# Lines layer of a four-layer scan stack: one padded copy by rows and one by columns, in place of one by rows for each of two images

## The chip, the cores and the metric

The kernel runs on one core of a Trainium2 chip. The metric is the device time of one launch, in microseconds. The kernel before takes 17721.58 us, the median of three runs that lie between 17714.92 and 17727.33 us.

## What is computed

The input is eight images of 48 x 48 pixels and 96 channels, float32. Four layers follow each other; each adds a function of the group-normed input to its input. Layers 0 and 3 are selective-scan blocks with a 3 x 3 convolution, layer 1 is a pointwise network between an up- and a downsampling, and layer 2, called the lines layer here, is the one that the change touches. It runs four independent scan blocks over the lines of the image: its rows forward, its rows backward, its columns forward and its columns backward.

```python
def _scan_block(x, in_w, conv_w, conv_b, xproj_w, dt_w, dt_b, A_log, D, outp_w):
    xz = x @ in_w
    xi, z = jnp.split(xz, 2, axis=-1)
    xc = jnp.pad(xi, ((0, 0), (K - 1, 0), (0, 0))).transpose(0, 2, 1)
    xconv = conv_general_dilated(xc, conv_w[:, None, :], ...)   # 4 taps along the line, per channel
    xi = jax.nn.silu((xconv + conv_b[None, :, None]).transpose(0, 2, 1))
    x_dbl = xi @ xproj_w
    dt_low, Bm, Cm = jnp.split(x_dbl, [DT_RANK, DT_RANK + D_STATE], axis=-1)
    dt = jax.nn.softplus(dt_low @ dt_w + dt_b)
    A = -jnp.exp(A_log)
    y = _selective_scan(xi, dt, A, Bm, Cm, D)    # h = exp(dt A) h + dt B u;  y = C h + D u
    y = y * jax.nn.silu(z)
    return y @ outp_w

b, h, w, c = x.shape
x_hf = x.reshape(b * h, w, c)
x_hb = x_hf[:, ::-1]
x_v = x.transpose(0, 2, 1, 3).reshape(b * w, h, c)
x_vb = x_v[:, ::-1]
ys = jax.vmap(_scan_block)(jnp.stack([x_hf, x_hb, x_v, x_vb]), in_w, conv_w, ...)
# the four results are turned back, concatenated and multiplied by out_w; out_b is added
```

Here x has been group-normed (32 groups of three channels), there are 192 inner channels and 16 states, and the result is added to the layer's input.

## The kernel before, in words

The program works through layer 0, then layer 2, then layer 3, each image by image. Layer 1 has no stretch of its own: as a "guest" it is strewn in small pieces into the slots of layers 0 and 2.

In the lines layer (`lines`, from line 772) channels lie on the partitions. An image is taken in four directions, k = 0 and 1 along rows, k = 2 and 3 along columns, and each direction in five blocks of ten lines (the last of eight), 480 or 384 positions. So an image is 20 blocks. A block is eight slots, or four turns of two slots. In a turn VectorE (DVE) runs three scans (L331) over 128 partitions x 2 x 480 positions. ScalarE (ACT) makes their decays with an exp (`make_da`, L323), and copies of B into PSUM (L280). VectorE and GpSimd (POOL) multiply `dt u` by B (L299), GpSimd multiplies the scanned states by C (L337), and TensorE (PE) sums them over states into `ps_y` (`reduce`, L357 and L359). When a half's `ps_y` is complete, VectorE multiplies it by the gate (`done`, L919), TensorE projects it (L928) and VectorE adds it to the image in SBUF (L934, L936).

What a block needs before its scans is made ahead, by `stage1`, three blocks early. The dictionary at its end says in which slot each step is issued; counted from the start of the block two before it, the convolution of the first half is in slot 3, of the second half in slot 4, and the gate's matmuls (`s7`, L897) in slot 1 of the next block. ACT has silus in slots 6 and 2 and a softplus in slot 0, each with a table load, and one more to return to exp.

The convolution and the input projection are one: four matmuls, one for each tap, read the normed image at four offsets (L854), and the gate reads it at offset zero (L897). A float32 matmul is two instructions in the profile. For that the normed image lies in `xpad`, with three zeros between lines of 48 (`step` is 51) and three lines of zeros above and below. There are two such tiles, for even and odd images, both laid out by rows. Where the direction is along columns, `shifted` turns the view around:

```python
def shifted(off):
    v = shift(xp, off, 0).rearrange("p h w -> p w h") if col else shift(xp, 0, off)
    return v[:, b.r0:b.r0 + b.nr, :]
```

so that neighbouring positions lie 51 elements apart.

The order of every engine's work is written out by hand; no scheduler moves it. In each slot `aside` issues, in this order: loads of B, C and dt, one step of `side`, the steps of `stage1`, postponed steps, and a piece of the guest. `side(job)` prepares the next image: in slot 8 of an image (or later, if layer 1 has not finished the next one) it issues the load of the next image on SyncE's queue, 28 slots later it starts `front`, whose statistics (`norm_scale`, L191 to L214) take 15 slots, and then writes the padded copy with five ACT instructions (L177), one per slot: slots 51 to 55 of 160. `load_x` uses two tiles in turn, so an image is loaded over the one before the present one. An image's result is stored by L938 after its last block.

Of the kernel before, what the change touches and what calls it, by code (L numbers as in the profile page):

```python
# [10 lines left out]
AF = mybir.ActivationFunctionType  # L11
# [4 lines left out]
H, W, C = 48, 48, 96  # L16
# [3 lines left out]
NK = 4  # L20
# [4 lines left out]
BLKS = [(0, 10), (10, 10), (20, 10), (30, 10), (40, 8)]  # L25
# [4 lines left out]
NG = 8  # L30
# [24 lines left out]
def seq(t, col):  # L55

    if len(t.shape) == 2:
        return t.rearrange("p (h w) -> p w h" if col else "p (h w) -> p h w", w=W)
    return t.rearrange("p a (h w) -> p a w h" if col else "p a (h w) -> p a h w", w=W)
# [42 lines left out]
def vss_stack_kernel(ctx: ExitStack, tc: tile.TileContext, i: dict, out: bass.AP):  # L102
    nc = tc.nc
# [11 lines left out]
    def weights(pool, names):  # L115
        w = {}
        for name in names:
            shape = list(i[name].shape)
            w[name] = pool.tile(shape, F32, tag=f"w_{name}", name=f"w_{name}")
            nc.sync.dma_start(w[name], i[name])  # L120
        return w
# [49 lines left out]
    def group_norm(x, into, psum, behind=lambda step: step()):  # L171


        got = {}
        yield from norm_scale(x, got, psum, behind)
        for r0, nr in BLKS:
            nc.scalar.activation(into(r0, nr), x[:, r0:r0 + nr, :], AF.Identity, bias=got["shift"], scale=got["rs"])  # L177
            yield True

    def norm_scale(x, got, psum, behind=lambda step: step()):  # L180


        def mean_of(v):
            def run():
                got["p"] = psum()
                nc.tensor.matmul(got["p"][:C, :1], lhsT=wc["gmat"], rhs=v, start=True, stop=True)
            behind(run)

        st = small.tile([C, 6, nc.vector.BN_STATS_DIM], F32, tag="st", name="st")
        for n in range(6):  # L190
            nc.vector.bn_stats(st[:, n, :], x[:, 8 * n:8 * n + 8, :])  # L191
            if n % 2:
                yield True
        mv = small.tile([C, 2], F32, tag="mv", name="mv")
        nc.vector.bn_aggr(mv, st)
        yield True
        mean_of(mv[:, 0:1])
        yield
        gm = small.tile([C, 1], F32, tag="gm", name="gm")
        nc.vector.tensor_copy(gm, got["p"][:C, :1])  # L200
        dev = small.tile([C, 1], F32, tag="dev", name="dev")
        nc.vector.tensor_sub(dev, mv[:, 0:1], gm)
        nc.vector.tensor_mul(dev, dev, dev)
        nc.vector.tensor_add(dev, dev, mv[:, 1:2])
        for _ in range(7):
            yield True
        mean_of(dev)
        yield
        rs = small.tile([C, 1], F32, tag="rs", name="rs", bufs=2)
        nc.scalar.activation(rs, got["p"][:C, :1], AF.Sqrt, bias=eps5[:C])  # L210
        yield True
        nc.vector.reciprocal(rs, rs)
        shift = small.tile([C, 1], F32, tag="shift", name="shift", bufs=2)
        nc.vector.scalar_tensor_tensor(shift, gm, -1.0, rs, ALU.mult, ALU.mult)  # L214
        got["rs"], got["shift"] = rs, shift
        yield True
# [270 lines left out]
    def sizes(b, half):  # L487

        return [b.dds[:, half, n, b.at] for n in range(2)]

    def make_room(b, pools):
        b.room = pools["dds"].tile([DH, LEAD + 4 * WMAX], F32, tag="dds", name="dds")
        b.dds = b.room[:, LEAD:LEAD + 4 * b.m].rearrange("p (h t m) -> p h t m", h=2, t=2)
# [279 lines left out]
    def lines(xin, xout, guest):  # L773
        stack = ExitStack()
        pools, ps = scan_pools(stack)
# [4 lines left out]
        xs = {}  # L780
# [8 lines left out]
        pad, step = 3, W + 3  # L789
        xpads = []  # L790
# [5 lines left out]
        def shift(t, dy, dx):  # L796

            at = (pad + dy) * step + pad + dx
            return t[:, at:at + H * step].rearrange("p (h w) -> p h w", w=step)[:, :, :W]

        def front(b, behind=lambda step: step()):
            xp = xpads[b % 2]
            yield from group_norm(seq(xs[b], False), lambda r0, nr: shift(xp, 0, 0)[:C, r0:r0 + nr, :], lambda: ps("sb", 1),
                                  behind)

        wide, part = square(wt, {"cw": NK * 4 * 2 * DH, "inz": 2 * NK * DH, "xp": 2 * NK * NBC, "dtw": 2 * NK * DH, "diag": 2 * NK * DH, "wo": 2 * NK * C})
        nc.sync.dma_start(part("inz"), i["l2_inz"].rearrange("p k c -> p (k c)"))
# [2 lines left out]
        w = weights(wt, [f"l2_{n}" for n in ("cb", "dtb", "a", "d", "outb")])  # L810
# [16 lines left out]
        for _ in front(0):  # L827
            pass
        for k in range(NK):
            nc.vector.tensor_mul(taps[:, k], taps[:, k], wl["l2_inu"][:, k].unsqueeze(1).to_broadcast([DH, 4, 2 * DH]))  # L830
            for half in range(2):
                nc.scalar.activation(diag[:, k, half, :], wc["ident"], AF.Identity, scale=w["l2_d"][:, k, half:half + 1])

                p = ps("sa" if half else "sb", 1)
# [3 lines left out]
        def stage1(b):  # L838
            n = b.n
            col, rev = dirs[b.k]  # L840
            xp = xpads[b.job % 2]
            got = {}

            def shifted(off):
                v = shift(xp, off, 0).rearrange("p h w -> p w h") if col else shift(xp, 0, off)
                return v[:, b.r0:b.r0 + b.nr, :]

            def conv(half):
                def run():
                    got["u", half] = ps("sa" if half else "sb", 1)  # L850
                    for tap in range(4):
                        off = tap - 3 if not rev else 3 - tap
                        at = ((b.k * 4 + tap) * 2 + half) * DH
                        nc.tensor.matmul(got["u", half][:, :n], lhsT=wide("cw", at),  # L854
                                         rhs=shifted(off), start=(tap == 0), stop=(tap == 3))
                return run

            def s2():
                b.uball = ubs[(len(BLKS) * (NK * b.job + b.k) + (len(BLKS) - 1 - b.blk if rev else b.blk)) % 3]
                b.uball = b.uball.rearrange("p (h n) -> p h n", h=2)  # L860
                b.ub = b.uball[:DH]
                for half in range(2):
                    nc.scalar.activation(b.ub[:, half, :n], got["u", half][:DH, :n], AF.Silu,  # L863
                                         bias=w["l2_cb"][:, b.k, half:half + 1])

            def s2s3():
                s2()
                s3()

            def s3():  # L870
                got["p"] = ps("sa", 1)
                for half in range(2):
                    nc.tensor.matmul(got["p"][:, :n], lhsT=wide("xp", (2 * b.k + half) * NBC), rhs=b.uball[:, half, :n],  # L873
                                     start=(half == 0), stop=(half == 1))

            def s4():
                b.bcl = pools["bcl"]
                nc.scalar.copy(b.bcl[:NBC, :n], got["p"][:NBC, :n])

            def s5():  # L880
                s4()
                for half in range(2):
                    got[half] = ps("sb" if half else "sa", 1)
                    nc.tensor.matmul(got[half][:, :n], lhsT=wide("dtw", (2 * b.k + half) * DH), rhs=b.bcl[:, :n],
                                     start=True, stop=True)

            def s6():
                nc.sync.dma_start(b.bcd, b.bcl[:2 * NS, :n])
                make_room(b, pools)
                for half in range(2):  # L890
                    nc.scalar.activation(sizes(b, half)[0], got[half][:DH, :n], AF.Softplus,
                                         bias=w["l2_dtb"][:, b.k, half:half + 1])

            def s7():
                for half in range(2):
                    got["z", half] = ps("sb" if half else "sa", 1)
                    nc.tensor.matmul(got["z", half][:, :n], lhsT=wide("inz", (2 * b.k + half) * DH),  # L897
                                     rhs=shifted(0), start=True, stop=True)
                make_du(b, b.ub[:, :, :n].rearrange("p h (r s) -> p h r s", s=SEG))
                for half in range(2):  # L900
                    store_dd(b, half)

            def s8():
                b.zb = up.tile([DH, 2, BMAX], F32, tag="zb", name="zb")
                for half in range(2):
                    nc.scalar.activation(b.zb[:, half, :n], got["z", half][:DH, :n], AF.Silu)

            return {3: conv(0), 4: conv(1), 6: s2s3, 7: s5, 8: s6, 9: s7, 10: s8}
# [4 lines left out]
        gated, tail = {}, []  # L913
# [26 lines left out]
            return [(1, project), (2, add)]  # L940

        def side(job):
            if job + 1 < nb:
                for _ in range(NG):
                    yield
                while guest.made <= job + 1:
                    for _ in range(NG):
                        yield
                load_x(job + 1)

                for _ in range(3 * NG + 4):
                    yield
                yield from front(job + 1, tail.append)

        dirs = DIRS_L2
        guest.banks = lambda slot, clear: {0: ["sa"], 2: ["sb"], 3: ["sa"], 6: ["sb"]}.get(slot, [])
# [270 lines left out]
    guest = Guest(stack, x1, x2)  # L1227
# [98 lines left out]
```

## Time and profile before

| what | value |
|---|---|
| median of three runs | 17721.58 us |
| the profiled execution's own time | 17729.41 us |
| its span, first to last instruction | 17727.6 us |
| instructions | 168890 |
| mean granted TensorE clock | 0.848 |
| busy: DVE, POOL, ACT, PE | 90, 86, 78, 78% of the span |
| first scan of the lines layer | 5956 us |
| first scan of layer 3 | 12280 us |
| L854, convolution matmuls, ps_sb | 1280 instructions, 892.9 us, 851 ns mean |
| L854, convolution matmuls, ps_sa | 1280 instructions, 865.3 us, 827 ns mean |
| L897, gate matmuls | 320 instructions, 279.8 us, 965 ns mean (ps_sa) |
| L177 into the padded copy, lines layer | 40 instructions, 674/788/798 ns (least, median, greatest) |

The profile is one execution. Its page gives busy time per engine over the whole span, so a stage has to be looked at by itself. Other views of the same trace give the busy time in chosen stretches, the instructions of one source line with their waits, the sum of waits by who waited for whom, and the instructions in order of time. A bracket in the timeline is idle time of the engine just before the instruction, and what ended it. Matmuls are pipelined: the duration of one is longer than the distance between two, so the length of a run of them says more than their mean.

### The profile page before, as it was taken

Reading aid. Unit: us, or ns where it says so; the run is one execution under the profiler, and the core shown is the slowest. Engines: PE = TensorE matmul, PEld = TensorE weight load, DVE = VectorE, ACT = ScalarE, POOL = GpSimd, SP = SyncE. Lnnn points to the kernel's source line nnn. Section 1 sums busy time; section 2 is a strip of 40 time slices with the busy share of each in tenths; the row PEclk is TensorE's granted clock in tenths of the full one; section 3 lists DMA queues with packets and bytes.
Section 4 is the critical chain, followed back from the end, with each engine's and each line's share of the span. In section 5 each row is a group of like instructions: output and inputs, shape, how many; then the busy total and the mean of one; then the engine's idle time right before and its main releaser. Section 6 shows DMA issues by size and latency. Waiting matters only on the chain.

```text
span 17727.6 us, 168890 instructions
## 1 busy us (share of the span) xinstructions
PE 13790.2 (78%) x53740; PEld 4743.1 (27%) x53740; DVE 15966.8 (90%) x9976; ACT 13871.7 (78%) x20932; POOL 15188.7 (86%) x8015
## 2 busy tenths in 40 slices
PE   6778787878787787888888887886777777777776
PEld 1223233323232322232222322222122222222221
DVE  7999999999899788888888889996999999999998
ACT  6878888878787677787777778785878778778776
POOL 7988888888888677777777778886999999999998
PEclk7878888989797888988889898998878878778877
DMA  4555545454545334443443444443445445455454
GB/s 139 180 166 172 175 167 173 168 178 171 170 167 177 130 132 158 137 153 143 150 145 137 151 149 154 152 151 123 172 172 175 171 172 178 169 174 177 169 176 143
DMA packets 887918, 2843.65 MB, mean 160 GB/s; under 512 B 353468, under 2 KB 421788, under 8 KB 760206
## 3 DMA queue, kind: packets, MB, share of 16 engines
q1 hardware_dynamic: 887022, 2832.85, 46.5%
q8 instruction: 422, 6.91, 0.2%
q14 instruction: 474, 3.88, 0.1%
HBM read 2384.40 MB, written 448.17 MB: 160 GB/s over the span
## 4 chain that ended last, share of the span: by engine, by line
PE 22%; ACT 19%; POOL 19%; DVE 18%; issue 13%; DMA 8%; SPq 1%; POOLq 0%; ACTq 0%; DVEq 0%
POOL dbu L337 12%; DVE dbu L331 12%; ACT ps_da L323 7%; DVE dbu L299 5%; POOL dbu L299 4%; PE ps_y L357 4%; PE ps_sb L854 3%; PE ps_sa L854 3%; DMA dd<-dds 3%; ACT L323 3%; POOL dds L499 2%; DMA dd<-dd 2%; ACT ps_b L280 1%; PE ps_sa L873 1%; PE ps_sa L928 1%
## 5 line engine op out<-in xcount | busy, mean ns | idle before, releaser
L331 DVE TENSOR_TENSOR_SCAN dbu<-ps_da,dbu 128x968 f32<-128x968 f32 (+3 forms) x5760 | 11821.9, 2074 | 859.4 <-ACT ps_da L323 709.1
L337 POOL TENSOR_TENSOR dbu<-dbu,bc 128x1440 f32<-128x1440 f32 (+1 forms) x3840 | 10070.9, 2635 | 2197.6 <-DVE dbu L331 2122.5
L323 ACT ACTIVATE ps_da<-dd,w_l_a 128x484 f32<-128x484 f32 (+3 forms) x11520 | 7426.5, 649 | 2560.3 <-DVE dbu L331 2331.3
L357 PE MATMUL ps_y<-dbu,w_red 128*32 128x480 f32 (+1 forms) x23040 | 4215.5, 654 | 1532.5 <-POOL dbu L337 1503.5
L359 PE MATMUL ps_y<-dbu,w_red 128*32 128x480 f32 (+1 forms) x7680 | 4178.0, 653 | 0.0
L299 DVE TENSOR_TENSOR dbu<-dd,ps_b 128x962 f32<-128x962 f32 (+5 forms) x2880 | 3828.4, 1329 | 251.7 <-ACT ps_b L280 157.5
L299 POOL TENSOR_TENSOR dbu<-dd,bc 128x481 f32<-128x481 f32 (+5 forms) x2240 | 3913.7, 1762 | 24.0 <-DMA dd<-dd 19.2
L357 PEld LDWEIGHTS ps_y<-dbu,w_red 128*32 128x32 f32 x23040 | 731.1, 118 | 5001.5 <-POOL dbu L337 3241.6
L280 ACT COPY ps_b<-bc 128x482 f32<-128x482 f32 (+3 forms) x2720 | 1448.8, 533 | 194.3 <-DVE dbu L299 152.0
L574 PE MATMUL ps_side<-xpad,w_l_cw 128*128 128x480 f32 (+1 forms) x2880 | 1337.6, 603 | 49.6 <-ACT g_room L1152 18.1
L323 ACT ACT_TABLE_LOAD x993 | 1274.0, 1283 | 17.8
L703 PE MATMUL ps_s<-bcl,square 128*128 128x480 f32 (+1 forms) x1280 | 885.1, 782 | 326.0 <-ACT dds L707 170.3
L854 PE MATMUL ps_sb<-xpad,square 128*128 128x480 f32 (+1 forms) x1280 | 892.9, 851 | 86.5 <-ACT g_room L1152 30.9
L353 PE MATMUL ps_y<-big,eye 128*128 128x480 f32 (+1 forms) x960 | 748.5, 868 | 237.1 <-ACT big L754 232.6
L713 PE MATMUL ps_s<-big,square 128*128 128x480 f32 (+1 forms) x1280 | 847.6, 793 | 65.6 <-ACT g_room L1152 18.5
L854 PE MATMUL ps_sa<-xpad,square 128*128 128x480 f32 (+1 forms) x1280 | 865.3, 827 | 0.0
L499 POOL TENSOR_TENSOR dds<-dds,big 96x960 f32<-96x960 f32 (+1 forms) x320 | 706.5, 2208 | 165.5 <-ACT dds L731 165.2
L574 PEld LDWEIGHTS ps_side<-xpad,w_l_cw 128*128 128x128 f32 x2880 | 568.0, 208 | 806.5 <-issue 696.3
L359 PEld LDWEIGHTS ps_y<-dbu,w_red 128*32 128x32 f32 x7680 | 667.8, 118 | 0.0
L897 PE MATMUL ps_sa<-xpad,square 128*128 128x480 f32 (+1 forms) x320 | 279.8, 965 | 295.4 <-ACT g_room L1152 99.6
L873 PE MATMUL ps_sa<-ub,square 128*128 128x480 f32 (+1 forms) x640 | 355.0, 686 | 194.8 <-ACT ub L863 194.8
L707 ACT ACTIVATE dds<-ps_s,w_l_dtb 96x480 f32<-96x480 f32 (+1 forms) x640 | 405.1, 633 | 125.7 <-DMA dd<-dds 82.0
(242 smaller groups left out, 12825.1 us busy)
## 6 DMA issues: line engine op xcount, KB each, us to landing
dd<-dd SPq DMA_DIRECT2D x512, 1452.0 KB
bc<-bcd SPq DMA_DIRECT2D x1536, 480.0 KB
dd<-dd SPq DMA_DIRECT2D x256, 1440.0 KB
dd<-dds SPq DMA_DIRECT2D x512, 363.0 KB
dd<-dd SPq DMA_DIRECT2D x128, 1164.0 KB
bc<-bcd SPq DMA_DIRECT2D x384, 384.0 KB
dd<-dds SPq DMA_DIRECT2D x256, 360.0 KB
dd<-dd SPq DMA_DIRECT2D x64, 1152.0 KB
```

The lines of the kernel that those rows point to most:

```text
L280: nc.scalar.copy(bps[t][:, :bcs[t][0].shape[1]], bcs[t][0])
L299: engine.tensor_mul(o, du, by.unsqueeze(1).to_broadcast([P, hi - lo, by.shape[1]]))
L323: nc.scalar.activation(da[:, at:at + b.m], b.got[half][:, u % 3, 0, :], AF.Exp, scale=a[:, b.k, ci:ci + 1])
L331: nc.vector.tensor_tensor_scan(db, da, db, 0.0, ALU.mult, ALU.add)
L337: nc.gpsimd.tensor_mul(h, h, bcs.pop(2 * t + sub)[1].unsqueeze(1).to_broadcast([P, 3, n]))
L357: nc.tensor.matmul(y[32 * g:32 * g + 32, :n], lhsT=wc["red"][:, :32], rhs=hc[:, g, b.at], start=False, stop=(slot == 3))
L359: nc.tensor.matmul(y[DH:, :n], lhsT=wc["red"][:, 32:], rhs=hc[:, 2, b.at], start=False, stop=(slot == 3))
L499: nc.gpsimd.tensor_mul(du, dt, u)
L574: nc.tensor.matmul(pu[:, :n], lhsT=flat[:, at:at + P], rhs=xpad[:, r0 + dy:r0 + dy + nr, dx:dx + W], start=(tap == 0), stop=(tap == 8))
L703: nc.tensor.matmul(got["p"][:, :n], lhsT=wide("dtw", (2 * b.k + half) * DH), rhs=b.bcl[:, :n], start=True, stop=True)
L713: nc.tensor.matmul(got["p"][:, :n], lhsT=wide("xp", (2 * b.k + half) * NBC), rhs=uall[:, half], start=(half == 0), stop=(half == 1))
L854: nc.tensor.matmul(got["u", half][:, :n], lhsT=wide("cw", at), rhs=shifted(off), start=(tap == 0), stop=(tap == 3))
```

## The change

The two padded tiles get other roles. `rowwise` holds the present image by rows; `colwise` holds it by columns. Directions along rows read the one, those along columns the other, each with neighbouring positions side by side. `rowwise` is still written by five ACT instructions from the normed image (now inside `front`), but as there is one such tile, for all images, they wait until slot 72, when the row directions of the present image have been read. `colwise` is filled by `turned`: five ACT copies out of `rowwise`, read across its rows, one per slot in slots 8 to 12 of the image. The load of the next image comes after them, in slot 16 at the earliest. The first image's `rowwise` is written before the scans, as was its padded copy.

```diff
-        def front(b, behind=lambda step: step()):
-            xp = xpads[b % 2]
-            yield from group_norm(seq(xs[b], False), lambda r0, nr: shift(xp, 0, 0)[:C, r0:r0 + nr, :], lambda: ps("sb", 1),
-                                  behind)
+        rowwise, colwise = xpads
+
+        def front(b, behind=lambda step: step(), wait=()):
+            got = {}
+            x = seq(xs[b], False)
+            yield from norm_scale(x, got, lambda: ps("sb", 1), behind)
+            yield from wait
+            for r0, nr in BLKS:
+                nc.scalar.activation(shift(rowwise, 0, 0)[:C, r0:r0 + nr, :], x[:, r0:r0 + nr, :], AF.Identity,
+                                     bias=got["shift"], scale=got["rs"])
+                yield True
+
+        def turned():
+
+            for r0, nr in BLKS:
+                nc.scalar.copy(shift(colwise, 0, 0)[:C, r0:r0 + nr, :],
+                               shift(rowwise, 0, 0)[:C].rearrange("p h w -> p w h")[:, r0:r0 + nr, :])
+                yield True
...
             def shifted(off):
-                v = shift(xp, off, 0).rearrange("p h w -> p w h") if col else shift(xp, 0, off)
-                return v[:, b.r0:b.r0 + b.nr, :]
+                return shift(colwise if col else rowwise, 0, off)[:, b.r0:b.r0 + b.nr, :]
...
         def side(job):
+            used = NG
+            for _ in range(NG):
+                yield
+            for clear in turned():
+                used += 1
+                yield clear
             if job + 1 < nb:
-                for _ in range(NG):
+                while guest.made <= job + 1 or used % NG:
+                    used += 1
                     yield
-                while guest.made <= job + 1:
-                    for _ in range(NG):
-                        yield
                 load_x(job + 1)
 
                 for _ in range(3 * NG + 4):
+                    used += 1
                     yield
-                yield from front(job + 1, tail.append)
+
+                def wait():
+                    nonlocal used
+                    used += 15
+                    while used < (NK // 2 * len(BLKS) - 1) * NG:
+                        used += 1
+                        yield
+                yield from front(job + 1, tail.append, wait())
```

More of the change, by code (lines that the diff above doesn't have):

```diff
@@ L840, in stage1 @@
             col, rev = dirs[b.k]
-            xp = xpads[b.job % 2]
             got = {}
             def shifted(off):
-                v = shift(xp, off, 0).rearrange("p h w -> p w h") if col else shift(xp, 0, off)
-                return v[:, b.r0:b.r0 + b.nr, :]
+                return shift(colwise if col else rowwise, 0, off)[:, b.r0:b.r0 + b.nr, :]
             def conv(half):
```

## The prediction

> **What bounds the kernel now.** I read the page first for the engines over the span, then the table of stretches for the lines layer alone, then the instructions that read `xpad`, then the waits of VectorE, then the timeline at one such wait.
>
> ```profile
> PE 13790.2 (78%) x53740; PEld 4743.1 (27%) x53740; DVE 15966.8 (90%) x9976; ACT 13871.7 (78%) x20932; POOL 15188.7 (86%) x8015
> ```
>
> VectorE is busiest, but this is a mean over three layers. The change touches only the lines layer, from 5956 us (its first scan) to some 12.1 ms; I cut at 12088 us, two blocks before its last scan. In that stretch, then in two row blocks (k=0) and two column blocks (k=2) of the third image:
>
> ```profile
> 5956.00:12088.00 6132.00, 5050.24 (x18084) 1709.33 (x18085) 5358.59 (x3433) 4819.17 (x7037) 4852.19 (x2211) 0.90 0.42 147
> ...
> 7551.00:7627.00 76.00, 59.22 (x249) 22.82 (x248) 68.12 (x42) 60.90 (x89) 63.10 (x28) 0.90 0.51 177
> ...
> 7890.00:7977.00 87.00, 75.64 (x249) 23.61 (x248) 69.36 (x42) 62.35 (x92) 63.61 (x29) 0.92 0.37 134
> ```
>
> The columns are the stretch, its length, busy time of PE, weight load, DVE, ACT and POOL, granted clock, DMA share and GB/s. With the same 249 matmul instructions and DVE work (68.1 and 69.4 us), the column blocks last 11 us longer and PE is busy 16 us more. The convolution's own instructions, row window (7551 to 7700) and column window (7890 to 8100):
>
> ```profile
> L854 PE MATMUL ps_sb<-xpad,square x32: 483/563/670, 7571.1 to 7687.3; 128*128 128x480 f32 x16, 128*128 128x384 f32 x16
> ...
> L854 PE MATMUL ps_sb<-xpad,square x40: 932/1120/1178, 7912.2 to 8088.2; 128*128 128x480 f32 x24, 128*128 128x384 f32 x16
> ```
>
> Same tile, same shapes: the median goes from 563 to 1120 ns. The waits of DVE in the same two windows (us, times, longest):
>
> ```profile
> DVE dbu L331 <- ACT ps_da L323: 7.5, 9, 1.6
> ...
> DVE gated L919 <- PE ps_y L359: 1.2, 2, 0.7
> ...
> DVE gated L919 <- PE ps_y L359: 15.7, 5, 4.0
> DVE dbu L331 <- ACT ps_da L323: 13.5, 13, 1.6
> DVE x L936 <- PE ps_sa L928: 8.5, 5, 2.3
> ```
>
> Once per block DVE stands some 3 us at `gated`, and PE is what ends it. The timeline, first a row block, then a column block:
>
> ```profile
> 7571.08 3.49 PE L854 MATMUL ps_sb<-xpad,square 128*128 128x480 f32 x8 [0.85 <-ACT g_room L1163]
> ...
> 7577.58 0.64 DVE L919 TENSOR_TENSOR gated<-zb,ps_y 96x480 f32<-96x480 f32 x1
> ...
> 7956.81 7.74 PE L854 MATMUL ps_sb<-xpad,square 128*128 128x480 f32 x8 [0.48 <-ACT g_room L1163]
> ...
> 7966.37 0.65 DVE L919 TENSOR_TENSOR gated<-zb,ps_y 96x480 f32<-96x480 f32 x1 [4.04 <-PE ps_y L359]
> ```
>
> Eight convolution instructions (four taps, two passes each) go through in 3.49 us by rows and 7.74 us by columns. Behind them in PE's queue stands the reduction that completes `ps_y`; DVE, with scans queued behind `gated`, waits 4.04 us.
>
> To size this I cut the layer at every third DVE scan: a turn, two slots; four turns are a block. Layer 1 runs as a guest in the first 110 of 160 blocks. For full-size blocks of the first five images (rows: blocks 18, 19, 0, 1; columns: 8 to 11, 16, 17), the turns last 11.0, 9.7, 8.0, 10.0 us by rows and 11.0, 10.3, 11.0, 10.5 by columns; PE is busy 7.4 and 7.0 us of row turns 2 and 3, but 10.4 and 10.4 in column ones. Turns 2 and 3 hold slots 4 to 7; the convolution stands in slots 3 and 4. So column blocks are PE-bound there, and nowhere else. DVE's idle time per guest block: columns 7.8 us (3.1 at `gated`, 1.6 at L936, 3.0 at scans), rows 3.65 us.
>
> [...] A column read steps 51 fp32 values[...] (0.97 us per instruction against 0.44, from 7.74/8 and 3.49/8). [...] For the padded writes (480 elements, two pointers) [...] the trace has a median of 788, and 1283 for a load.
>
> **The change, part by part.**
>
> *Column reads made contiguous.* 20 instructions per full column block (16 convolution, 4 gate L897): 0.53 us less each, some 10.5 us of PE time per block, of which the path sees what DVE waits for. In guest blocks the four waits should fall to the row level: 7.8 - 3.65 = 4.1 us. The block lengths say the same: columns average 41.8 us, rows 37.9 with the norm work in them. There are 52 such blocks: 52 x 4.1 = 213 us. Without the guest (28 column blocks) DVE waits 0.95 us at `gated`, but row turn 1 is no shorter there (9.2 against 8.8 us); I take half: 28 x 0.45 = 12 us. Together 225. Low end: only the `gated` wait goes, (3.14 - 0.36) x 52 = 145. High end: a least-squares fit of guest block lengths on convolution time gives 0.5 us per us, 0.5 x 10.5 x 52 = 273, and all 0.95 x 28 = 27: 300.
>
> *Copy by columns added.* Five ACT copies per image, 40 in all, one per slot in slots 8 to 12; the built order shows each where ACT also has its exps, with no wait of its own and no further table load. No SBUF copy with a strided read is in the trace. The nearest is L754, by rows and then by columns (strided write):
>
> ```profile
> L754 ACT COPY big<-ps_y x8: 547/548/549, 811.3 to 934.5; 96x480 f32<-96x480 f32 x8
> ...
> L754 ACT COPY big<-ps_y x6: 963/967/973, 985.9 to 1082.7; 96x480 f32<-96x480 f32 x6
> ```
>
> I take 0.97 us; [...] above, the padded write's 0.79 plus the same 0.42 for the stride, 1.2. Four of five fall into turns 0 and 1, where ACT does the softplus and gate tables: there it is busy 9.4 of 11.0 and 8.4 of 9.7 us, and scans wait for its `ps_da`. I charge 0.6 of them: 4 x 0.97 x 0.6 x 8 images = 19 us. If all five showed at 1.2 us: 48; if the slack swallows them: 0.
>
> *Padded writes moved.* Seven times five ACTIVATEs of 0.79 us go from slots 51 to 55 to 72 to 76. They sat mostly in turns 2 and 3 of block 6, which took 8.0 and 10.2 us with them and 7.8 and 10.1 in the last image, without. Now four are in turns 0 and 1 of block 9: three more in busy turns, 3 x 0.79 x 0.6 x 7 = 10 us (0 to 22). Statistics, two mean matmuls and the Sqrt with its two table loads move eight slots, same turns of the next block: nothing, as their cover (full DVE turns) is the same; bare they are some 3 us of DVE and 3 of ACT per image.
>
> *Load of x.* Eight slots later on SP's queue, past loads of `bc` and `dd`, and still 28 slots (some 134 us) ahead of use. The buffer it refills is stored in the previous block, now with eight more slots to spare. Nothing; were it late, DVE's statistics would wait. POOL's order is unchanged.
>
> *New reuse waits.* `rowwise` is rewritten from slot 72, its last reader (gate of block 9) issues in slot 65; `colwise` from slot 8, its last reader is in slot 145 of the image before: both long done.
>
> Sum: 225 - 19 - 10 = 196 us off. Against the profiled execution (17729.4 us; span 17727.6) that is 17533; the median of the runs is 7.8 us lower, so 17526.
>
> **Rivals.** *The next bound takes it.* With PE free, column turns 0 and 1 are already ACT's (9.6 of 11.0) and POOL's (9.9 of 10.3 us), and the new copies land there. If only the `gated` wait goes and ACT's work mostly shows: 145 - 55 = 90, giving 17632. For it: scans waiting on ACT are the largest wait of DVE. Against: row blocks carry the same ACT and POOL work and are 4 us shorter. *More comes free:* guest evictions on ACT wait for PE too, and the fit's 0.5 holds with little ACT cost: 300 - 15, giving 17437. *Slower:* ACT's copies in turns 0 and 1 are exposed and PE's relief is not on the path: 48 + 22 = 70, giving 17792. It decides only if relief is below the ACT cost; the 4.04 us wait speaks against it. *It doesn't do what it says:* column matmuls stay slow for another reason than stride (clock): then +29, 17751. Against: granted clock is 0.92 in the column stretch, 0.90 in the row one.
>
> **How the numbers follow.** Forecast 0.68 (own range 17480 to 17575), next bound 0.14, more 0.12, slower 0.04, no effect 0.02. Slow-side tails take the range to 17632, the fast side to 17445: together 8 in 10. Faster by over 0.2% (35 us, about what a measurement of this kernel can tell): 0.93, from the first three less a tail; within it 0.02; slower 0.05.
>
> **What would show it.** Right: column L854 at 563 ns median; the `gated` wait in the lines layer from 216 us to under 60; guest column blocks near 38 us; 40 copies near 0.97 us; block 1 longer by 2 to 3 us, block 6 shorter and block 9 bearing the writes. Wrong: copies over 1.3 us with scans waiting for ACT in blocks 1 and 9; or column blocks staying above 40 us with PE idle, the wait passed to ACT or POOL.

## The result, and the profile after

The changed kernel takes 17467.10 us (median of four runs, 17465.38 to 17468.38), the kernel before 17718.25 us beside it (four runs, 17711.60 to 17727.33): 251 us less, a ratio of 0.9858 with a 95% interval of 0.9841 to 0.9875. The forecast was 17526 us, 196 us less; the result lies inside the whole range set (17445 to 17632), but below the forecast's own (17480 to 17575).

Cut at the first scan of each layer, the two profiled executions (spans 17727.6 and 17465.4 us) differ like this:

| stretch | before | after | difference |
|---|---|---|---|
| layer 0 | 5956.1 | 5970.0 | +13.9 |
| lines layer | 6324.0 | 6052.7 | -271.3 |
| layer 3 | 5447.5 | 5442.7 | -4.8 |

Layers 0 and 3 run the same instructions in both; what they differ by here is variation from one execution to the next.

The page's busy times after:

```profile
PE 13240.6 (76%) x53740; PEld 4749.1 (27%) x53740; DVE 15969.0 (91%) x9976; ACT 13903.6 (80%) x20972; POOL 15179.8 (87%) x8015
```

PE is busy 550 us less with the same number of instructions; ACT has 40 more. In what follows, as in the prediction, a "column block" is a block in whose slots a convolution by columns is issued. That runs two blocks ahead of the scans, so these are blocks 8 to 17 of each image: 52 with the guest and 28 without. The other ten are called row blocks.

The table of stretches, for the lines layer, then row blocks 0 and 1 and column blocks 9 and 10 of the third image (the blocks shown of before):

```profile
5970.00:11833.00 5863.00, 4475.67 (x18086) 1709.35 (x18086) 5356.87 (x3434) 4851.51 (x7077) 4848.17 (x2211) 0.88 0.44 154
7478.00:7556.00 78.00, 59.79 (x246) 22.64 (x245) 69.13 (x42) 66.86 (x97) 63.86 (x28) 0.89 0.45 161
7812.00:7887.00 75.00, 58.83 (x250) 23.16 (x249) 68.85 (x43) 65.52 (x97) 63.87 (x28) 0.91 0.43 156
```

The two column blocks went from 87 to 75 us, with DVE's busy time the same (69.4 and 68.9) and PE's down from 75.6 to 58.8. The two row blocks went from 76 to 78: block 1 now carries the copies (ACT 60.9 before, 66.9 after). The granted clock is no higher than before (0.88 in the lines layer, against 0.90), so it is not what made PE faster. The convolution by columns (now line L866), in the window 7812 to 8020:

```profile
L866 PE MATMUL ps_sb<-xpad,square x48: 483/564/670, 7833.5 to 8018.1; 128*128 128x480 f32 x32, 128*128 128x384 f32 x16
```

564 ns is the row figure. The waits of DVE in the lines layer, before and after, both from 5970 to 12000 us (before, this leaves out the last four blocks; after, it takes in the setup of layer 3):

```profile
DVE dbu L331 <- ACT ps_da L323: 349.8, 315, 2.8
DVE gated L919 <- PE ps_y L359: 213.4, 87, 6.3
DVE x L936 <- PE ps_sa L928: 122.3, 84, 3.5
```

```profile
DVE dbu L331 <- ACT ps_da L323: 259.1, 244, 3.3
DVE x L948 <- PE ps_sa L940: 118.7, 99, 2.4
...
DVE gated L931 <- PE ps_y L359: 24.5, 20, 5.4
```

The wait at `gated` (now L931) is nearly gone, and the scans' wait for ACT fell by 91 us as well, which I had counted in part, through the row level. ACT itself waited for PE less: for the guest's matmuls (into `g_room`) 323 us before and 184 after, and for the convolution (`ub`) 53 us before and none after. The timeline at the very place shown of before, block 10 of the third image:

```profile
7871.78 3.49 PE L866 MATMUL ps_sb<-xpad,square 128*128 128x480 f32 x8 [0.48 <-ACT g_room L1187]
...
7877.21 0.62 DVE L931 TENSOR_TENSOR gated<-zb,ps_y 96x480 f32<-96x480 f32 x1
```

The eight instructions of the first half take 3.49 us in place of 7.74 (0.44 each in place of 0.97; a single one is recorded with 564 ns here and 1120 before, so the records of neighbours overlap), and `gated` follows without a wait in place of one of 4.04 us.

### The profile page after: what moved, and what is told of

It reads as the page before. It is cut to its first block, busy times and chain, and to the rows that moved or that the text cites. A ratio compares the mean times of both kernels' runs of the same rounds, so it can differ in the third digit from the quotient of the medians.

```text
span 17465.4 us, 168933 instructions
## 1 busy us (share of the span) xinstructions
PE 13240.6 (76%) x53740; PEld 4749.1 (27%) x53740; DVE 15969.0 (91%) x9976; ACT 13903.6 (80%) x20972; POOL 15179.8 (87%) x8015
## 4 chain that ended last, share of the span: by engine, by line
DVE 22%; ACT 21%; POOL 19%; issue 14%; PE 13%; DMA 10%; SPq 1%; POOLq 0%; DVEq 0%; ACTq 0%
DVE dbu L331 14%; POOL dbu L337 12%; ACT ps_da L323 7%; DVE dbu L299 6%; POOL dbu L299 5%; DMA dd<-dds 4%; DMA dd<-dd 3%; ACT L323 3%; PE ps_y L357 2%; POOL dds L499 2%; ACT ps_b L280 1%; PE ps_sa L940 1%; PE ps_sa L885 1%; DMA bc<-bcd 1%; ACT L903 1%
## 5 line engine op out<-in xcount | busy, mean ns | idle before, releaser
L885 PE MATMUL ps_sa<-ub,square 128*128 128x480 f32 (+1 forms) x640 | 405.0, 770 | 382.9 <-ACT ub L875 382.9
L866 PE MATMUL ps_sb<-xpad,square 128*128 128x480 f32 (+1 forms) x1280 | 600.5, 615 | 85.0 <-ACT g_room L1176 31.3
L866 PE MATMUL ps_sa<-xpad,square 128*128 128x480 f32 (+1 forms) x1280 | 538.0, 561 | 0.0
L754 ACT COPY big<-ps_y 96x480 f32<-96x480 f32 (+1 forms) x640 | 471.0, 736 | 34.7 <-PE ps_y L359 33.3
```

## The experiments

Times are medians, each beside runs of the kernel before on the same chip. For the mechanism I also compare block lengths in the lines layer: the stretches outside it, the same in all these kernels, differ by up to 30 us between profiled executions (layer 0 took 5951 to 5981 us), while block sums inside repeat closely (the changed kernel's lines layer took 6052.7 and 6054.8 us in two profiles).

**Contiguous reads alone.** Two theories: A, the relief is larger than forecast and the additions on ACT cost the forecast 29 us; B, the relief is as forecast and the re-timing of the next image's load and statistics gave the rest.

```diff
-                v = shift(xp, off, 0).rearrange("p h w -> p w h") if col else shift(xp, 0, off)
-                return v[:, b.r0:b.r0 + b.nr, :]
+                return shift(xp, 0, off)[:, b.r0:b.r0 + b.nr, :]
```

> The kernel before, but the column directions read the padded copy as if by rows (contiguous), with no copy by columns and nothing moved; the column directions then compute on rows, the work is the same in number and size. It has the relief of TensorE alone. Theory A (relief was sized too small, ACT's additions cost the forecast 29 us): about 280 us faster than before. Theory B (relief was right, the re-timing of the next image's load and statistics gave the rest): about 225 us faster. If stride is not the cause: within 35 us of before.

17460.81 us against 17729.60: 269 us less, ratio 0.9851 (0.9836 to 0.9866). The relief alone is as much as the whole change (251 us less above, 262 less in the repeat below), and nearer to A's 280 than to B's 225, which lies outside the interval. In the lines layer (6041.5 us) column blocks lose 265.7 us in sum and row blocks 16.8.

**Taps alone.** The gates' matmuls keep the strided read.

```diff
-            def shifted(off):
-                v = shift(xp, off, 0).rearrange("p h w -> p w h") if col else shift(xp, 0, off)
+            def shifted(off, turn=False):
+                v = shift(xp, off, 0).rearrange("p h w -> p w h") if turn and col else shift(xp, 0, off)
...
-                                     rhs=shifted(0), start=True, stop=True)
+                                     rhs=shifted(0, True), start=True, stop=True)
```

> The kernel before, but only the convolution taps of the column directions read contiguously, as if by rows; the gate's matmuls keep the strided read; nothing is copied or moved. The column directions' convolution then computes on rows. If the convolution in slots 3 and 4 is what holds back the sum that DVE's gated waits for: the gated wait goes from some 3.1 to under 0.5 us per column block, and 190 to 240 of the 269 us of the run with contiguous reads remain. If the gates (2.5 us per block, in slot 1) carry a share as large as their time: about 200.

17476.71 against 17734.31 us: 258 less, 0.9858 (0.9843 to 0.9873). The two waits concerned, in the same window as above:

```profile
DVE x L936 <- PE ps_sa L928: 130.0, 92, 3.2
...
DVE gated L919 <- PE ps_y L359: 32.8, 27, 5.4
```

The `gated` wait fell (0.18 us per column block with the guest, 3.14 before) and the wait at L936 stayed. 258 us is more than the 190 to 240 expected: the convolution carries nearly all, and the rival that gave the gates a share by their time (about 200 us left) is out. By block lengths the gates are worth some 20 us (lines layer 6062.1 against 6041.5), which end-to-end times don't resolve.

**The strided read in the row directions too.**

```diff
-                v = shift(xp, off, 0).rearrange("p h w -> p w h") if col else shift(xp, 0, off)
+                v = shift(xp, off, 0).rearrange("p h w -> p w h") if True else shift(xp, 0, off)
```

> The kernel before with the row directions, too, reading the padded copy in steps of 51, as the column ones do (they then compute on columns); nothing else changes. If the strided read in slots 3 and 4 is the cause, row blocks with the guest go from 37.9 us to about the column blocks' 41.8 (58 blocks, 3.9 to 4.6 us each), those without by about 1 us (22 blocks): 245 to 290 us slower than before. If column directions are slower for another reason (column adds, their place in the image): within 35 us.

17991.77 against 17723.36 us: 268 more, 1.0150 (1.0133 to 1.0167). Row blocks with the guest went from 37.91 to 41.72 us on average, beside 41.89 for column blocks. So the cost is the stride's, not the column direction's.

**The strided convolution later in the queue.** Is it the place ahead of the sum, or PE's time?

```diff
-            return {3: conv(0), 4: conv(1), 6: s2s3, 7: s5, 8: s6, 9: s7, 10: s8}
+            return {4: conv(0), 5: conv(1), 6: s2s3, 7: s5, 8: s6, 9: s7, 10: s8}
```

> The kernel before, reads still strided, with the two halves of the convolution issued in slots 4 and 5 in place of 3 and 4, for all directions: in slot 4 the first half stands behind the sum that gated waits for, no longer ahead of it. If the place in TensorE's queue is what costs (and not its busy time as such): the gated wait of column blocks falls from 3.1 to under 1 us, but the silu in slot 6 now waits for the convolution, with the exps behind it, and part is given back: 30 to 150 us faster. If TensorE's throughput is what costs: no gain, or slower.

17801.37 against 17723.36 us: 78 more, 1.0043 (1.0028 to 1.0058). A miss. The waits of DVE and then of ACT in the window 5970 to 12000:

```profile
DVE dbu L331 <- ACT ps_da L323: 587.6, 341, 7.7
...
DVE gated L919 <- PE ps_y L359: 14.7, 9, 3.8
```

```profile
ACT ps_da L323 <- DVE dbu L331: 628.7, 667, 7.0
ACT ub L863 <- PE ps_sa L854: 276.3, 72, 6.7
```

The `gated` wait nearly vanished (213.4 to 14.7 us), so that wait comes from the place ahead of the sum. But the silu's wait for the convolution rose to 276.3 us (53.2 before), and the exps queued behind it on ACT made the scans wait 238 us more. In full column blocks with the guest, turn 2 fell from 11.0 to 7.8 us and turn 3 rose from 10.5 to 13.3, PE busy all of it. Over the 52 column blocks with the guest this nearly cancels (19 us less in sum). The loss is in the 28 without it: 94 us more, as turn 3 went from 10.3 to 14.7 us, PE again busy all of it. So the time did not come back with the wait, and the outcome is the one that was set down for PE's throughput: in column blocks with the guest PE is busy 20.3 of the 20.9 us of turns 2 and 3 before, and 20.2 of 20.5 here. There the place only decides which engine waits, and PE's own time, with two strided halves of 7.7 us each ahead of the silu in slot 6, decides how long the two turns last; without the guest the later place costs by itself. Other places were not tried.

**The additions, one by one, on the kernel before.** First the load of the next image in slot 16 and its statistics from slot 44:

```diff
-                for _ in range(NG):
+                for _ in range(2 * NG):
                     yield
                 while guest.made <= job + 1:
```

> The kernel before with one change: the load of the next image in slot 16, so that its statistics start in slot 44 and its padded copy is written in slots 59 to 63. Theory A: within 10 us of before. Theory B: 15 to 25 us faster, since statistics no longer fall into the short blocks 4 and 5.

Then the padded writes at slots 72 to 76 on top of it (`front` as in the change, but into its image's own tile):

```diff
+            yield from wait
             for r0, nr in BLKS:
...
-                yield from front(job + 1, tail.append)
+                yield from front(job + 1, tail.append, (None for _ in range(13)))
```

> As the run with late statistics, and the five padded writes wait until slots 72 to 76, where the changed kernel has them. Against that run it shows what the place of the writes costs. Theory A (forecast): 10 us slower than the run with late statistics, 22 at most. Theory B: no difference beyond 5 us.

And the timing of the first of these with the 40 copies ("the next run" in the quoted text is the late statistics one):

```diff
+        def turned(job, col=True):
+            here, there = shift(xpads[job % 2], 0, 0)[:C], shift(xpads[(job + 1) % 2], 0, 0)[:C]
+            v = here.rearrange("p h w -> p w h") if col else here
+            for r0, nr in BLKS:
+                nc.scalar.copy(there[:, r0:r0 + nr, :], v[:, r0:r0 + nr, :])
+                yield True
...
+            for _ in range(NG):
+                yield
+            yield from turned(job, True)
             if job + 1 < nb:
-                for _ in range(NG):
+                for _ in range(NG - len(BLKS)):
                     yield
```

> The kernel before with its strided column reads, plus the 40 ACT copies across rows in slots 8 to 12 (into the other padded tile, where the next image's rows later overwrite them; nobody reads them), and the load of x in slot 16, statistics from slot 44 as in the changed kernel. Against the next run (same timing, no copies) it shows the bare cost of the copies. Theory A: 19 to 30 us slower than that one. Theory B: under 10 us. The copies take 1.11 us each, as in the changed kernel.

| kernel | time | ratio to before | lines layer |
|---|---|---|---|
| late statistics | 17742.95 | 1.0004 (0.9996 to 1.0012) | 6322.2 |
| late statistics, late writes | 17728.62 | 0.9999 (0.9991 to 1.0007) | 6312.5 |
| late statistics, copies | 17746.48 | 1.0007 (0.9999 to 1.0015) | 6331.1 |

None can be told from before (17729.60 us, lines layer 6324.0), so the 15 to 25 us that B gave to the re-timing are out. Blocks 4 and 5 do get 18 us shorter over eight images, but blocks 6 to 8 get 23 longer. Nor does A's cost for the writes show (10 us expected; the lines layer is 10 shorter). The copies cost 9 us of the lines layer, which is B's range (under 10) and below A's 19; block 1 alone grows by 11 us over eight images. So A was right on the relief, and B on the small cost of the additions.

**Can the copies be placed better?** The changed kernel beside two variants: copies in slots 4, 5, 6, 7, 12 and writes in 76 to 79 and 84; and the same writes with the copies on POOL in slots 6, 6, 7, 7, 14.

```diff
             for r0, nr in BLKS:
+                for _ in range(4 if wait and r0 == 40 else 0):
+                    yield
...
-            used = NG
-            for _ in range(NG):
-                yield
-            for clear in turned():
-                used += 1
-                yield clear
+            used, copies = 0, turned()
+            for slot in (4, 5, 6, 7, 12):        # with POOL: (6, 6, 7, 7, 14)
+                while used < slot:
+                    used += 1
+                    yield
+                next(copies)
...
-                    while used < (NK // 2 * len(BLKS) - 1) * NG:
+                    while used < (NK // 2 * len(BLKS) - 1) * NG + 4:
...
-                nc.scalar.copy(shift(colwise, 0, 0)[:C, r0:r0 + nr, :],
+                nc.gpsimd.tensor_copy(shift(colwise, 0, 0)[:C, r0:r0 + nr, :],   # with POOL
```

> The changed kernel once more, beside the next three on one chip: 245 to 260 us faster than before.

> The changed kernel with its copies in slots 4, 5, 6, 7 and 12 and its padded writes in slots 76 to 79 and 84: in turns 2 and 3, where ACT has most time to spare, in place of turns 0 and 1. Theory A (additions in the table turns cost what block 1 grew by, 11 us, and up to 7 in block 9): 10 to 18 us faster than the changed kernel. Theory B (the copies' cost is made up for by other waits): within 5 us of it.

> As the run before (writes in light turns), with the copies by columns on POOL, in slots 6, 6, 7, 7 and 14, where POOL is busy some 5.5 of 9.5 us. If POOL's slack takes them, block 1 shrinks to its length before the change and the kernel is as fast as the contiguous reads alone, 10 to 18 us faster than the changed kernel. If a POOL copy with a strided read takes over 2.5 us, the last turn of block 0 grows and the gain is gone.

| kernel | time | ratio to before | lines layer | blocks 0 and 1, eight images, against before |
|---|---|---|---|---|
| changed, again | 17471.95 | 0.9853 (0.9837 to 0.9870) | 6054.8 | +10 |
| light turns | 17482.28 | 0.9859 (0.9845 to 0.9874) | 6056.4 | +14 |
| copies on POOL | 17471.11 | 0.9854 (0.9840 to 0.9869) | 6043.1 | +0.5 |

All three are the same by their times. The light turns were a miss: with them blocks 0 and 1 cost no less, and block 0's last turn, which had no copy in it in the changed kernel, took 11.8 us against 11.1 before. On POOL blocks 0 and 1 are back at their old length and the lines layer is 12 us shorter than the changed kernel's beside it, but no gain shows in the time: neither variant is shown to beat the change.

The copies themselves, on ACT in the changed kernel, then on POOL:

```profile
L816 ACT COPY xpad<-xpad x40: 922/1114/1133, 6013.2 to 11247.9; 96x480 f32<-96x480 f32 x32, 96x384 f32<-96x384 f32 x8
```

```profile
L818 POOL COPY xpad<-xpad x40: 922/1112/1142, 6000.0 to 11242.5; 96x480 f32<-96x480 f32 x32, 96x384 f32<-96x384 f32 x8
```

## Why the prediction was right, and where its sizes were off

*The bound and the mechanism* were right: column blocks were held by PE in turns 2 and 3, through a strided convolution standing ahead of the sum that `gated` waits for. The taps-only and the all-strided run show that the strided convolution is the cause. The later-taps run shows that its place ahead of the sum makes the `gated` wait, but that moving it away gains nothing while PE's time in turns 2 and 3 stays.

*Relief in guest blocks*, forecast 52 x 4.1 = 213 us. With contiguous reads alone the 52 column blocks went from 41.81 to 37.23 us: 238. Of the 25 us between them, some 10 lie in the yardstick: I let column blocks fall to the row blocks' idle time of before, 3.65 us, and DVE's idle time in them fell from 7.87 to 3.45. Those rows were not undisturbed: blocks 7 and 18 were the idlest, with 4.9 us each; the one follows the padded writes, the other holds the last column gate (with contiguous reads it fell to 3.0). The rest is rounding (4.22 taken as 4.1, 6 us) and 0.16 us per block in which DVE was busy less (8 us).

*Relief without the guest*, forecast 12: 28 blocks from 36.92 to 35.93, 28 us. Halving it, because row turn 1 was no shorter, was wrong: PE was busy 8.5 of 8.5 and 10.1 of 10.3 us in turns 2 and 3 of these blocks, so they were PE-bound there too; the prediction had read PE's busy time by turn for blocks with the guest only.

*Row blocks*, forecast nothing: 17 us, 10 of them in blocks 18 and 19. The last column gate is issued in block 18, so a part of this may be relief too; that was not tested apart.

*The copies*: the price was too low (0.97 us taken, 1.11 measured, under the 1.2 set as its upper end), the exposure too high (0.6 of four; 8 x 1.35 us, a quarter of the 5.4 us of copying per image, measured in block 1). Forecast 19 us, measured 9 to 11 in the lines layer.

*The moved writes*: forecast 10 us; none measured. *Statistics, load, reuse waits*: forecast nothing, and none shows in the times.

Together: relief 225 forecast and 282 measured by blocks (269 by times), additions 29 forecast and 11 to 13 measured by blocks (the changed kernel's lines layer in two profiles, less that of contiguous reads alone). So two terms were mis-sized, and both errors have one sign, which is why the time fell 59 us below the forecast. The rival "more comes free" named a larger relief (up to 300) and a small ACT cost; its 17437 us is nearer to the measured time (30 us off) than the forecast. Its reason, guest evictions on ACT that wait for PE, shows in the waits above (323 to 184 us), but how much of the relief came that way is not shown.

*What should show it*: L866 at 564 ns, the `gated` wait under 60 us, guest column blocks near 38 us (37.38) and a longer block 1 (1.35 us, not 2 to 3) all came. Block 6 did not get shorter (+0.65 us): the padded writes and the Sqrt left it, but small DVE steps of the statistics (4.4 us together) came into its first turn, which went from 9.7 to 13.0 us. The forecast had put them at nothing; over blocks 4 to 8 their shift nearly evens out (18 us less and 23 more with late statistics alone).

## What to carry to other kernels

What a doubled matmul costs is not read from the engine's mean over the span (78% here), but from the turns in which that engine is never idle: look for the wait that ends at it, and count how often it comes. To move the slow work in the queue may only hand the wait to another engine, as in the later-taps run (`gated` 213 to 15 us, the silu 53 to 276). Turning the operand once, with 40 copies of 1.1 us, made the reads of 1600 matmul instructions contiguous, and the copies showed with a quarter of their time; why not more is not shown, since in turns where ACT has more time to spare they cost as much (14 us in blocks 0 and 1 with the light turns, 10 in the changed kernel beside it). To size what a relief gives, use an undisturbed stretch as the yardstick, not one with other work in it, and look for the bound in every kind of block.

## What the runs showed of the hardware

A read of float32 in steps of 51 elements took nearly the same time on three engines. From the mean durations of the 480- and the 384-element form: PE (1128 - 942) / 96 = 1.94 ns per element and pass (L854 before, columns, window 7890 to 8100), against (577 - 497) / 96 = 0.83 contiguous (L866 after, window 7812 to 8020); ACT (1117 - 936) / 96 = 1.89 (L816 after). On POOL the same 40 copies took 922 to 1142 ns, with a median of 1112, beside 922 to 1133 and 1114 on ACT. I had expected ACT's copy to cost what L754's strided write does (0.97 us). The runs show the size of the stride's cost; what in the memory or the engines causes it was not shown.
